# A Perceiver kernel with 64 sequences: context layer norm on VectorE, scores between turned weights and values, first sequences interleaved

## The chip, the cores and the metric

The kernel runs on one core of a Trainium2 chip. The metric is the device time of one execution in microseconds. A core has five engines that run side by side, each through its own queue in order: TensorE (PE, matmuls; PEld are its weight loads), VectorE (DVE), ScalarE (ACT), GpSimd (POOL), and SyncE (SP), which issues most of the DMAs. Matmul results land in PSUM, which the kernel uses as eight banks of 128 x 512 float32.

## What is computed

The reference is two Perceiver layers on `x` (64 sequences of 32 latent tokens, 256 channels) with a context of 257 tokens per sequence. Everything is float32. Cut to what matters here:

```
x += xattn0(layernorm(ctx)*gx+bx, layernorm(layernorm(x))*gl+bl)  # 16 heads of 64; keys and values from
                                                 # context and latents; q and k normed per head
x += attn0(layernorm(x))                         # 16 heads of 16, q and k normed per head
x += moe(layernorm(x))                           # 64 experts, top 8, capacity 128, plus a shared expert
x += xattn1(layernorm(x), ctx)                   # 16 heads of 64
x += attn1(layernorm(x))                         # latent heads of 32, rotary, causal
x += tanh(layernorm(x) @ w @ a1 @ a2 + bias)
```

## The kernel before

Tokens stand in 16 tiles `t` of 128, so a tile holds four sequences (`NB = 4`), and a sequence `s` is number `b = s % 4` of its tile. The program has three parts, called stages here.

**First stage (`before`)**: cross-attention of layer 0 sequence by sequence, and beside it, for tiles that are done, self-attention and routing. For each sequence `CrossFirst` has these steps: `load` (DMA of 256 context rows), `prepare` (layer norm of the context), `turn` (transposition on TensorE, line 1173, and copies to `xT`), `keys` (16 products with `wk`, copies to `kT` by VectorE and ScalarE in turn, and two ScalarE squares `sq` of four head pairs each, line 1206), `norms` (matmuls that sum the squares, line 1218, then a maximum and a logarithm, `nk`), `spread` (matmuls that spread the norms over the rows, line 1239, then four exponentials), `scores` (line 1258, then softmax on VectorE and ScalarE), `weigh` (turns the softmax weights, line 207, copies `at`, line 208), and `values` (line 221, copies `yT`). One pass of the loop works on several sequences: `keys(s+2)`, `weigh(s)`, a slot, `norms(s+2)`, `values(s)`, `spread(s+2)`, a slot, `turn(s+3)`, `scores(s+2)`, `prepare(s+4)`, and, except for a tile's last sequence, a third slot. In a slot every open generator does its next step, up to its next `yield`. A tile's generator `tail` runs `heads_out`, then `self_first` with `attend_self` (line 310 are its values' matmuls, 32 x 32 each), then `route`, which ends in eight indirect DMAs on POOL that scatter the tokens to their experts. The generator `queries` prepares the next tile. The last tile but one is held back by `HOLD` slots.

**Second stage (`experts`)**: 64 experts, with their weights loaded `AHEAD = 12` ahead, and the shared expert between them. In expert 12 the weights of the third stage are loaded and folded (`after_weights`): `latent_weights` and `ffn_weights` each use a temporary pool on the same side of the memory.

**Third stage (`after`)**: layer 1, with `CrossSecond` for the cross-attention and the generator `follow` for output heads, self-attention (`self_second`) and FFN. A pass of the loop is: load, `scores(s+2)`, a slot, `weigh(s)`, a slot, `values(s)`, a slot. The generator `queries(t+2)` joins in the third pass of a tile. `normed`, which both use, makes a layer norm `z` in one step and its transpose `zT` (line 149, copy on line 150) in a later one.

**What sets the order.** The order on TensorE is that of the program (`manual_schedule` for PE). For the other engines and the DMA queues a scheduler picks the order by its own estimate of times; it also chooses between ScalarE and VectorE where the program says `nc.any`, and it may issue a load early once its buffer is free. All PSUM tiles come from one pool of eight banks:

```python
return self.ps.tile([P, 512], F32, name=name, tag="bank")
```

Of the kernel before, what the change touches and what calls it, by code (L numbers as in the profile page):

```python
# [14 lines left out]
ALU = mybir.AluOpType  # L15
AX = mybir.AxisListType

P = 128
D = 256
# [12 lines left out]
AHEAD = 12  # L32
# [54 lines left out]
def done(steps):  # L87
    for _ in steps:
        pass


class Kernel:
# [198 lines left out]
    def attend_self(self, t, e, recip, wo, bias):  # L291

        nc = self.nc
        v = self.vz[t % 2]
        nc.vector.tensor_tensor(e, e, recip.unsqueeze(2).to_broadcast([P, H, S]), ALU.mult)  # L295
        eT = self.wk.tile([P, H, S], F32, name="eT", bufs=self.eb)
        nc.vector.transpose(eT.rearrange("p a b -> p (a b)"), e.rearrange("p a b -> p (a b)"))
        yield
        if self.slack:
            yield  # L300


        ps = [self.bank("psY") for _ in range(NB)]
        for k in range(2):
            for odd in range(2):
                for g in range(4):
                    h = 8 * k + 2 * g + odd
                    for b in range(NB):
                        r = slice(b * S, (b + 1) * S)
                        nc.tensor.matmul(  # L310
                            ps[b][g * 32 : (g + 1) * 32, k * S : (k + 1) * S],
                            lhsT=v[r, h, :, :].rearrange("p a b -> p (a b)"),
                            rhs=eT[r, h, :],
                            start=(odd == 0),
                            stop=(odd == 1),
                        )
        oT = self.wk.tile([P, 2, P], F32, name="oTs", bufs=self.vb)
        for b in range(NB):
            nc.any.tensor_copy(
                oT[:, :, b * S : (b + 1) * S], ps[b][:, : 2 * S].rearrange("p (k i) -> p k i", k=2)  # L320
            )
        yield
        ps = self.bank("psY")
        self.product(ps[:, :D], [oT[:, k, :] for k in range(2)], [wo[:, k, :] for k in range(2)])
        self.add_to_x(t, ps[:, :D], bias)
# [46 lines left out]
    def before(self, ctx):  # L372
# [3 lines left out]
        tc, nc, a = self.tc, self.nc, self.a  # L376
# [3 lines left out]
        w = self.pool(ctx, "w0", 1)  # L380
# [11 lines left out]
        cross = CrossFirst(self, kp)  # L392
# [23 lines left out]
        n = self.nb  # L416
        first = cross.queries(0)
# [2 lines left out]
        next(first)  # L420
        next(first)
        cross.prepare(1)
        for i in range(2):
            cross.load(i + 2)
            cross.turn(i)
            cross.keys(i)
            cross.norms(i)
            done(first)
            cross.spread(i)
            cross.scores(i)  # L430
        cross.load(4)
        cross.prepare(2)
        cross.prepare(3)
        cross.turn(2)

        wv = self.load(w, "wv", [P, 2, HD], a["a_wv"].rearrange("(k p) n -> p k n", p=P))
        wo = self.load(w, "wo", [P, 8, D], a["a_wo"].rearrange("(k p) n -> p k n", p=P))
# [218 lines left out]
    def experts(self, ctx, slot, tails):  # L656
        tc, nc, a = self.tc, self.nc, self.a
        nt = self.nt
        w = self.pool(ctx, "w1", 1)
# [5 lines left out]
        def weigh(e):  # L665
            if e < E:
                t = weights[e] = wk.tile([P, 3 * D], F32, name="we", bufs=AHEAD + 1)
                nc.sync.dma_start(t, a["m_ew"][e])

        def fetch(e):  # L670
            if e < E:
                t = rows[e] = wk.tile([P, D], F32, name="be", bufs=4)
                nc.sync.dma_start(t, self.buf[1 + e * CAP : 1 + (e + 1) * CAP, :])

        def turn(e):
            if e < E:
                t = wk.tile([P, 2, P], F32, name="beT")
                self.transposed(t, rows.pop(e))
                mid[e] = t

        def inner(e):
            if e < E:
                t, we = mid.pop(e), weights[e]
                ps = self.bank("psA")
                for half in range(2):
                    self.product(
                        ps[:, half * P : (half + 1) * P],
                        [we[:, k * D + half * FI : k * D + (half + 1) * FI] for k in range(2)],
                        [t[:, k, :] for k in range(2)],
                    )  # L690
                act = mid[e] = wk.tile([P, P], F32, name="eact")
                nc.scalar.activation(act, ps[:, :P], AF.Silu)
                nc.vector.tensor_tensor(act, act, ps[:, P : 2 * P], ALU.mult)

        def outer(e):
            ps = self.bank("psY")
            self.product(ps[:, :D], [mid.pop(e)], [weights.pop(e)[:, 2 * D :]])
            oe = wk.tile([P, D], F32, name="oe")
            nc.any.tensor_copy(oe, ps[:, :D])
            nc.scalar.dma_start(self.oute[1 + e * CAP : 1 + (e + 1) * CAP, :], oe)  # L700
# [50 lines left out]
        for e in range(E):  # L751
            weigh(e + AHEAD)
            fetch(e + 3)
            turn(e + 2)
            while (at - total + rest) * E < rest * e:
                next(side)
                at += 1
            inner(e + 1)
            outer(e)
            if e == AHEAD:  # L760
                self.after_weights()
        done(side)

        side, sums = shared(nt // GT - 1), self.combine(0)
# [32 lines left out]
    def after_weights(self):  # L797
        a, w = self.a, self.w2
        wq = self.load(w, "wq", [P, 2, HD], a["b_wq"].rearrange("(k p) n -> p k n", p=P))
        wkT = self.load(w, "wkT", [P, 8, D], a["b_wkT"].rearrange("(k p) n -> p k n", p=P))  # L800
        wv = self.load(w, "wv", [P, 2, HD], a["b_wv"].rearrange("(k p) n -> p k n", p=P))
        wo = self.load(w, "wo", [P, 8, D], a["b_wo"].rearrange("(k p) n -> p k n", p=P))
        bo = self.row(w, "bo", a["b_bo"], D)
        self.weights = wq, wkT, wv, wo, bo
        self.lat = self.latent_weights(w)
        self.ffnw = self.ffn_weights(w)

    def after(self, ctx):
        self.eb = self.vb = 1
        self.slack = True  # L810
        nc, n = self.nc, self.nb
        wq, wkT, wv, wo, bo = self.weights
        self.wk = self.wkh = self.pool(ctx, "wk2", 2)
        kp = self.pool(ctx, "kp2", 3)
        cross = CrossSecond(self, kp, wq, wkT, wv, wo, bo)
        for s in range(3):
            cross.load(s)
        second = self.combine(1)
        for _ in range(6):
            next(second)  # L820
        done(cross.queries(0))

        steps = []

        def slot():
            for g in list(steps):
                if next(g, steps) is steps:
                    steps.remove(g)

        cross.scores(0)  # L830
        done(second)
        steps.append(cross.queries(1))
        slot()
        cross.scores(1)
        slot()
        steps.append(self.combine(2, 3))
        for s in range(n):
            t, b = divmod(s, NB)
            if s + 3 < n:
                cross.load(s + 3)  # L840
            if s + 2 < n:
                cross.scores(s + 2)
            if b == NB - 2 and t + 2 < self.nt:
                steps.append(cross.queries(t + 2))
                if t + 3 < self.nt:
                    steps.append(self.combine(t + 3, 3))
            slot()
            cross.weigh(s)
            slot()
            if s < 2:  # L850

                slot()
                slot()
            cross.values(s)
            if b == NB - 1:
                steps.append(self.follow(t, cross.yT, wv, wo, bo))
            slot()
        while steps:
            slot()
# [110 lines left out]
    def self_second(self, t, wl, bl, wvo, bvo, wqk, bqk, wo, bo):  # L970
        nc = self.nc
# [43 lines left out]
        kT = self.wk.tile([P, 4 * P], F32, name="kTl", bufs=1)  # L1015
        nc.any.tensor_copy(kT, ps)
        yield


        ps = [self.bank("psB") for _ in range(4)]  # L1020
# [12 lines left out]
        e = self.wk.tile([P, H, S], F32, name="e", bufs=self.eb)  # L1033
# [45 lines left out]
class CrossFirst:  # L1079
# [76 lines left out]
    def prepare(self, s):  # L1156

        k, nc, cx = self.k, self.k.nc, self.cx[s]
        k.layernorm(cx, cx)
        nc.gpsimd.tensor_tensor(cx, cx, self.gx.unsqueeze(1).to_broadcast([P, 2, D]), ALU.mult)  # L1160
        nc.gpsimd.tensor_tensor(cx, cx, self.bx.unsqueeze(1).to_broadcast([P, 2, D]), ALU.add)

    def turn(self, s):

# [307 lines left out]
```

## Time and profile before

| | |
|---|---|
| median of three runs | 2828.25 us (2827.0 to 2829.42) |
| time of the profiled execution | 2804.67 us |
| its span, first to last instruction | 2802.8 us |
| mean granted TensorE clock | 0.982 |
| PE busy | 2657.6 us (95%) |
| DVE busy | 1694.9 us (60%) |
| ACT busy | 1241.6 us (44%) |
| POOL busy | 684.3 us (24%) |

The first stage lasts until about 1550 us of the span, the second until about 1800, the third to the end. Busy shares are averages over these stages. A row of the timeline has start, duration, engine, line, operation, what it writes and reads, its shape, its count, and in brackets the idle time of the engine before it with what ended it. In a row of the waits stand who waited for whom, the total in us, how often, and the longest. A group of instructions has its busy time in us and the mean in ns of one. The durations come from one profiled execution.

### The profile page before, as it was taken

How to read it: one execution, taken by the hardware profiler on the slowest of the kernel's cores; microseconds unless marked ns; L12 is line 12 of the kernel's file. 1: busy time of each engine (PE TensorE's matmuls, PEld its weight loads, DVE VectorE, ACT ScalarE, POOL GpSimd, SP SyncE). 2: the span in 40 equal slices, each digit the busy share in tenths (PEclk: the TensorE clock that was granted, in tenths of full speed). 3: DMA queues.
4: the chain of work that ended last, by engine and by line, in shares of the span. 5: the costliest groups of instructions: out<-in, count | busy, mean ns of one | idle time of the engine just before them, and what ended most of it. 6: DMA issues, size and time to landing. Idle time of an engine off the chain costs nothing. (4 is left out here: it accounts for less than half of the span.)

```text
span 2802.8 us, 58905 instructions
## 1 busy us (share of the span) xinstructions
PE 2657.6 (95%) x23386; PEld 1824.5 (65%) x23386; DVE 1694.9 (60%) x4427; ACT 1241.6 (44%) x3436; POOL 684.3 (24%) x756
## 2 busy tenths in 40 slices
PE   6999999999999999999999799999999999999996
PEld 3556666666666666666666578667777777777764
DVE  5546666666666666666665433466666666666664
ACT  3455555555555555555554223333333333333331
POOL 5211333133313331243121200321212222121001
PEclk8999999999999999999999899999999999999997
DMA  8000011011000000000001677321211222222110
GB/s 271 16 14 18 31 33 31 18 31 33 29 18 27 26 22 18 20 19 16 18 7 38 233 237 243 91 67 54 58 51 50 59 52 58 56 51 55 33 35 5
DMA packets 136087, 157.03 MB, mean 56 GB/s; under 512 B 24024, under 2 KB 118979, under 8 KB 135812
## 3 DMA queue, kind: packets, MB, share of 16 engines
q1 hardware_dynamic: 114308, 119.65, 13.8%
q0 software_dynamic: 12288, 25.21, 3.4%
q10 hardware_dynamic: 9216, 8.39, 0.9%
q8 instruction: 185, 3.03, 0.4%
q14 instruction: 90, 0.74, 0.1%
HBM read 121.63 MB, written 37.75 MB: 57 GB/s over the span
## 5 line engine op out<-in xcount | busy, mean ns | idle before, releaser
L167 PE MATMUL psA<-xT,wk 128*128 128x289 f32 x2048 | 517.4, 411 | 7.9 <-ACT xT L1176 4.5
L167 PEld LDWEIGHTS psA<-xT,wk 128*128 128x128 f32 x2048 | 388.0, 191 | 134.8 <-issue 21.8
L780 POOL DMA_INDIRECT y<-oute,idx x128 | 131.5, 1028 | 643.4 <-DVE x L791 453.9
L167 PE MATMUL psA<-at,cx 128*128 128x512 f32 x512 | 235.4, 602 | 20.0 <-ACT qTl L1005 18.2
L221 PE MATMUL psY<-at,cx 128*128 128x512 f32 x512 | 239.8, 612 | 0.1
L167 PE MATMUL psY<-xT,qk 128*128 128x257 f32 x1024 | 234.3, 382 | 0.0
L167 PEld LDWEIGHTS psY<-xT,qk 128*128 128x128 f32 x1024 | 190.8, 190 | 35.0 <-issue 10.2
L1357 DVE TENSOR_REDUCE mx<-psY 128x1 f32<-128x257 f32 x256 | 105.7, 423 | 133.6 <-PE psY L167 133.5
L1358 ACT ACTIVATE sim<-psY,mx 128x257 f32<-128x257 f32 x256 | 121.6, 476 | 142.3 <-DVE mx L1357 142.2
L184 ACT ACTIVATE sim<-sim,mx 128x289 f32<-128x289 f32 x256 | 134.1, 526 | 100.0 <-DVE mx L182 100.0
L221 PEld LDWEIGHTS psY<-at,cx 128*128 128x128 f32 x512 | 93.5, 192 | 123.0 <-issue 108.8
L167 PEld LDWEIGHTS psA<-at,cx 128*128 128x128 f32 x512 | 92.9, 190 | 120.8 <-issue 76.7
L233 ACT COPY yT<-psY 128x512 f32<-128x512 f32 x127 | 68.2, 589 | 220.7 <-PE psY L231 220.7
L645 POOL DMA_INDIRECT buf<-z,fi x128 | 126.5, 988 | 148.0 <-DVE fi L642 102.2
L1160 POOL TENSOR_TENSOR cx<-cx,a_gx 128x512 f32<-128x512 f32 x64 | 81.8, 1278 | 292.1 <-DVE cx L140 290.3
L1206 ACT ACTIVATE sq<-kT 128x1156 f32<-128x1156 f32 x128 | 149.4, 1167 | 4.4 <-DVE kT L1203 2.8
L1201 ACT COPY kT<-psA 128x289 f32<-128x289 f32 x256 | 94.8, 389 | 104.2 <-PE psA L167 104.2
L1376 ACT COPY at<-psT 128x512 f32<-128x512 f32 x145 | 78.8, 595 | 123.4 <-PE psT L1375 118.3
L1218 PE MATMUL psB<-sq,c 128*32 128x289 f32 x1024 | 109.4, 419 | 19.7 <-ACT sq L1206 19.5
L1388 DVE SCALAR_TENSOR_TENSOR yT<-at,xT,psA 128x512 f32<-128x512 f32 x128 | 94.0, 735 | 56.1 <-PE psA L167 50.7
L167 PE MATMUL psY<-yT,wv 128*64 128x128 f32 x2048 | 121.6, 275 | 1.6 <-DVE yT L1388 1.4
L1177 POOL COPY xT<-lnT 128x64 f32<-128x64 f32 x64 | 15.3, 240 | 423.0 <-PE psA L167 299.3
(257 smaller groups left out, 5190.5 us busy)
## 6 DMA issues: line engine op xcount, KB each, us to landing
cx<-in_ctx SPq DMA_DIRECT2D x128, 256.0 KB
we<-in_m_ew SPq DMA_DIRECT2D x64, 384.0 KB
xT<-in_ctxT SPq DMA_DIRECT2D x64, 257.0 KB
buf<-zero SPq DMA_DIRECT2D x32, 256.0 KB
be<-buf SPq DMA_DIRECT2D x64, 128.0 KB
oute<-oe ACTq DMA_DIRECT2D x64, 128.0 KB
mu<-in_mask SPq DMA_DIRECT2D x16, 128.5 KB
x<-in_x SPq DMA_DIRECT2D x16, 128.0 KB
```

What stands on the lines that cost most here:

```text
L167: self.nc.tensor.matmul(ps, lhsT=lhs[i], rhs=rhs[i], start=(i == 0), stop=(i == n - 1))
L184: nc.scalar.activation(sim[:, g, :], sim[:, g, :], AF.Exp, bias=mx[:, g : g + 1], accum_out=sm[:, g : g + 1])
L221: nc.tensor.matmul(ps[kc], lhsT=values[i][:, kc * P : (kc + 1) * P], rhs=at[i], start=(i == 0), stop=(i == n - 1 and tail is None),)
L645: d = nc.gpsimd.indirect_dma_start(out=self.buf[:, :], out_offset=bass.IndirectOffsetOnAxis(ap=fi[:, k : k + 1], axis=0), in_=z[:, 0, :], ...
L780: nc.gpsimd.indirect_dma_start(out=y, out_offset=None, in_=self.oute[:, :], in_offset=bass.IndirectOffsetOnAxis(ap=self.idx[:, t, k : k + ...
L1160: nc.gpsimd.tensor_tensor(cx, cx, self.gx.unsqueeze(1).to_broadcast([P, 2, D]), ALU.mult)
L1201: nc.scalar.copy(kT[:, p, :], ps[:, :JK])
L1206: nc.scalar.activation(sq[p // 4], kT[:, p - 3 : p + 1, :], AF.Square)
L1218: nc.tensor.matmul(ps[g * 32 : (g + 1) * 32, :JK], lhsT=k.pair[odd], rhs=sq[p // 4][:, p % 4, :], start=(odd == 0), stop=(odd == 1),)
L1357: nc.vector.tensor_reduce(mx[:, g : g + 1], ps[:, :J], AX.X, ALU.max, negate=True)
L1358: nc.scalar.activation(sim[:, g, :], ps[:, :J], AF.Exp, bias=mx[:, g : g + 1], accum_out=sm[:, g : g + 1])
L1388: nc.vector.scalar_tensor_tensor(self.yT[:, c, :, b * S : (b + 1) * S], self.at[:, 2, :].rearrange("p (h i) -> p h i", h=H), xT[:, c, J - ...
```

## The change

The change has six parts. `prepare` takes mean and scale from `stats` and ends the layer norm with four `scalar_tensor_tensor` of 128 x 256 on VectorE, where two `tensor_scalar` on VectorE and a multiplication and an addition of 128 x 512 on GpSimd stood. `attend_self` gives up its slot once more in the first stage before line 310 (the third stage had that yield already). Before the first stage's loop the first two sequences are interleaved and three contexts are loaded at once. `ffn_weights` moves from expert 12 to expert 24. In the third stage `scores(s+2)` stands behind `weigh(s)` and no longer ahead of the pass's first slot. `self_second` gives up its slot once more before its scores (line 1026).

```diff
--- before.py
+++ after.py
@@ -296,8 +296,7 @@
         eT = self.wk.tile([P, H, S], F32, name="eT", bufs=self.eb)
         nc.vector.transpose(eT.rearrange("p a b -> p (a b)"), e.rearrange("p a b -> p (a b)"))
         yield
-        if self.slack:
-            yield
+        yield
 
 
         ps = [self.bank("psY") for _ in range(NB)]
@@ -420,18 +419,22 @@
         next(first)
         next(first)
         cross.prepare(1)
-        for i in range(2):
-            cross.load(i + 2)
-            cross.turn(i)
-            cross.keys(i)
-            cross.norms(i)
-            done(first)
-            cross.spread(i)
-            cross.scores(i)
-        cross.load(4)
+        for i in range(2, 5):
+            cross.load(i)
+        cross.turn(0)
+        cross.keys(0)
+        done(first)
+        cross.turn(1)
+        cross.norms(0)
         cross.prepare(2)
+        cross.spread(0)
+        cross.scores(0)
+        cross.keys(1)
+        cross.turn(2)
+        cross.norms(1)
         cross.prepare(3)
-        cross.turn(2)
+        cross.spread(1)
+        cross.scores(1)
 
         wv = self.load(w, "wv", [P, 2, HD], a["a_wv"].rearrange("(k p) n -> p k n", p=P))
         wo = self.load(w, "wo", [P, 8, D], a["a_wo"].rearrange("(k p) n -> p k n", p=P))
@@ -759,6 +762,8 @@
             outer(e)
             if e == AHEAD:
                 self.after_weights()
+            if e == 2 * AHEAD:
+                self.ffnw = self.ffn_weights(self.w2)
         done(side)
 
         side, sums = shared(nt // GT - 1), self.combine(0)
@@ -803,7 +808,6 @@
         bo = self.row(w, "bo", a["b_bo"], D)
         self.weights = wq, wkT, wv, wo, bo
         self.lat = self.latent_weights(w)
-        self.ffnw = self.ffn_weights(w)
 
     def after(self, ctx):
         self.eb = self.vb = 1
@@ -838,14 +842,14 @@
             t, b = divmod(s, NB)
             if s + 3 < n:
                 cross.load(s + 3)
-            if s + 2 < n:
-                cross.scores(s + 2)
             if b == NB - 2 and t + 2 < self.nt:
                 steps.append(cross.queries(t + 2))
                 if t + 3 < self.nt:
                     steps.append(self.combine(t + 3, 3))
             slot()
             cross.weigh(s)
+            if s + 2 < n:
+                cross.scores(s + 2)
             slot()
             if s < 2:
 
@@ -1015,6 +1019,7 @@
         kT = self.wk.tile([P, 4 * P], F32, name="kTl", bufs=1)
         nc.any.tensor_copy(kT, ps)
         yield
+        yield
 
 
         ps = [self.bank("psB") for _ in range(4)]
@@ -1156,9 +1161,11 @@
     def prepare(self, s):
 
         k, nc, cx = self.k, self.k.nc, self.cx[s]
-        k.layernorm(cx, cx)
-        nc.gpsimd.tensor_tensor(cx, cx, self.gx.unsqueeze(1).to_broadcast([P, 2, D]), ALU.mult)
-        nc.gpsimd.tensor_tensor(cx, cx, self.bx.unsqueeze(1).to_broadcast([P, 2, D]), ALU.add)
+        mv, rs = k.stats(cx, 2)
+        for j in range(2):
+            x = cx[:, j, :]
+            nc.vector.scalar_tensor_tensor(x, x, mv[:, j, 0:1], self.gx, ALU.subtract, ALU.mult)
+            nc.vector.scalar_tensor_tensor(x, x, rs[:, j : j + 1], self.bx, ALU.mult, ALU.add)
 
     def turn(self, s):
 
```

## The prediction, made before the changed kernel ran

> **What bounds the kernel now.** I read the page first: TensorE is busy nearly throughout, so only its gaps can be won, and whatever is moved out of a gap is lost.
>
> ```profile
> PE 2657.6 (95%) x23386; PEld 1824.5 (65%) x23386; DVE 1694.9 (60%) x4427; ACT 1241.6 (44%) x3436; POOL 684.3 (24%) x756
> ```
>
> Then TensorE's waits in the steady part of the first stage (210 to 1470 us): what waited, for whom, total us, times, longest.
>
> ```profile
> PE psY L310 <- DVE at L208: 14.7, 14, 1.3
> PE psB L1218 <- ACT sq L1206: 9.6, 14, 0.9
> ```
>
> The values' matmuls of self-attention (L310) wait 1.0 us once per tile, for PSUM banks that VectorE still empties. That looks like free time. The timeline of one such iteration (the last sequence of a tile; start, duration, idle before) shows where it sits: turning of weights (L207), L310, key norms (L1218).
>
> ```profile
> 516.41 1.47 PE L207 MATMUL psT<-c,sim 128*128 128x128 f32 x12
> 517.82 0.26 PE L310 MATMUL psY<-eT,vz 32*32 32x32 f32 x6
> 519.10 1.24 PE L310 MATMUL psY<-eT,vz 32*32 32x32 f32 x122 [1.03 <-DVE at L208]
> 520.27 1.86 PE L1218 MATMUL psB<-sq,c 128*32 128x289 f32 x16
> ```
>
> ScalarE in the same iteration, the two squares that the norms read:
>
> ```profile
> 517.13 1.15 ACT L1206 ACTIVATE sq<-kT 128x1156 f32<-128x1156 f32 x1
> ...
> 519.74 1.17 ACT L1206 ACTIVATE sq<-kT 128x1156 f32<-128x1156 f32 x1
> ```
>
> The second ends at 520.91. The norms' first four matmuls (0.44 us) could start at the turns' end (517.88), but the other twelve need that square: they start 0.05 us after it, 3.07 us after the turns' end, and all 14 such iterations show the same to 0.3 us. So the square sets the end here, and L310 with its wait fills the hole before it. What the hole looks like when empty stands in the last sequence of the first tile, which has no self-attention beside it:
>
> ```profile
> 143.42 0.68 PE L1218 MATMUL psB<-sq,c 128*32 128x289 f32 x4
> 146.20 1.26 PE L1218 MATMUL psB<-sq,c 128*32 128x289 f32 x12 [2.10 <-ACT sq L1206]
> ```
>
> and what follows there, cross-attention's values, otherwise 3.70 us for eight:
>
> ```profile
> 147.39 5.26 PE L221 MATMUL psY<-at,cx 128*128 128x512 f32 x8
> ```
>
> In the view by windows the granted clock is 0.5 from 147.14 to 150.56 us: 1.56 us lost after a gap of 2.10 us.
>
> Third stage, one tile: the values wait once per tile for copies on ScalarE (12 tiles, 18.2 us in all); below it a transposed z (L149), today followed by scores.
>
> ```profile
> 2132.73 3.67 PE L167 MATMUL psA<-at,cx 128*128 128x512 f32 x8 [1.50 <-ACT qTl L1005]
> ...
> 2137.53 0.38 PE L149 MATMUL psT<-c,z 128*128 128x128 f32 x2
> ```
>
> Drain and second stage: what a consumer directly behind such a transposition pays, and the wait for the FFN weights.
>
> ```profile
> 1542.53 0.38 PE L149 MATMUL psT<-c,z 128*128 128x128 f32 x2
> 1543.37 0.66 PE L167 MATMUL psA<-gw,zT 128*128 128x65 f32 x4 [0.46 <-ACT zT L150]
> ...
> 1633.27 3.75 PE L167 MATMUL psA<-f_a,f_a1T 128*128 128x256 f32 x8 [4.80 <-DMA f_a<-in_f_a]
> 1636.82 2.86 PE L167 MATMUL psA<-mid,f_wT 128*128 128x256 f32 x8
> ```
>
> Costs of the layer norm's instructions, old and nearest to the new (busy us, mean ns):
>
> ```profile
> L140 DVE TENSOR_SCALAR cx<-cx,mv,rs 128x256 f32<-128x256 f32 x128 | 61.8, 515 | 7.4 <-ACT rs L120 7.4
> ...
> L791 DVE SCALAR_TENSOR_TENSOR x<-y,w,x 128x256 f32<-128x256 f32 x128 | 59.8, 467 | 0.3
> ```
>
> **The change part by part**, against the profiled execution (2804.67 us, span 2802.8; the three runs' median is 2828.25, so I carry the difference over in us).
>
> *One more yield before L310, first stage.* A tile has 11 slots: three per sequence, two for the last. L310 is the tail's tenth step, in the last sequence's slot between turns and norms. It moves one slot on, behind the spread matmuls; later steps move one slot each (product with wo to the next sequence's first slot, then z's turn, gate, count). No DMA moves but zs's store and the scatters on POOL, one slot later; POOL has at most 28 us of work in 70 and TensorE waits for it nowhere here. Now the norms stand directly behind the turns, and their end stays at the square: values still start 4.17 us after the turns. Queued on TensorE behind the waiting norms are values, spread and scores, for which VectorE (nk, then the scores' products) waits in turn, so no other engine uses the hole. L310's 1.42 us (517.82 to 520.27 less 1.03) come out of the hole and are added behind the spread, plus a bank wait like that of L573, which has this place today (2.7 us in 14, 0.19 each), less 0.06 us of wait that the moved count matmuls fill: 1.55 us by 14 tiles = +21.7. Bounds: -12.0, if the square were early and only L310's 14.7 us less 2.7 counted, to +25.
>
> *Clock after the emptied hole.* 0.5 us idle, 0.44 busy, 2.2 idle. [...] of six gaps of 1.98 to 2.39 us outside the end, at full clock (from 53.67, 118.94, 144.10, 1535.06, 1544.03, 1603.30), four were followed by half clock. I take 0.7 by 1.5 us by 14 = +14.7; ends 0 and +21.
>
> *Layer norm on VectorE.* Per sequence two L140 (0.515) and POOL's multiplication and addition (1.28 and 1.27) go; four scalar_tensor_tensor come, by L791 0.467 each: 1.87 - 1.03 = +0.84 us of VectorE, 64 times, 54 us beside an engine 64% busy. POOL's 163 us were off the path, each sequence being prepared an iteration or more ahead. VectorE's queue counts: two of four preparations per tile stand at 569.0 to 571.9, among the copies of turned weights that the values read (last copy 1.60 us after the turns, values at 1.91). Behind them wait these copies and the norms' maximum. [...] POOL keeps one of 3.64 us (mask) and one of 1.92 us (q) per tile. [...] L140 today shows 0.1 us of excess over z's 0.41, so I stay with the rows. On the path I take +3 (0.2 us a tile); ends -1 and +12.
>
> *Start.* keys(1) no longer waits for its turn (0.68 us), but norms(1) still waits for ScalarE's second square at 55.6, behind the softmax of sequence 0. What goes is the turn of sequence 2 and its copy between scores(1) and keys(2) (62.3 to 64.3 us): -2.0, with q's chain freed from POOL -0.8, and spread(0) losing the transposes of q ahead of it +0.5: -2.3. Two cx loads pass four small c3 copies in SP's queue; both landed long before use. Half clock from 54.98 to 68.64 remains, since its waits do; were it gone, -6 more. Ends -8 and +4.
>
> *FFN weights 12 experts later.* Four loads and 16 matmuls move. The loads wait for the memory of the latent weights, free at 1628.1; SP issued later weights up to 36 us ahead of their place, so they pass the queue of expert weights and land long before. The 4.80 us go, and the slow clock behind it (3.75 + 2.86 against twice 1.89): -7.6. Ends: -7.6, and +1 if they keep their place behind expert loads that wait for a slot.
>
> *Third stage.* Scores (16 matmuls, their reduces, exponentials, scaling; no DMA) come between turns and values: the 18.2 us go. But the slots at the end of one iteration and the start of the next now touch. Two consumers stand there directly behind their transposed z: the latent projection (second sequence) and the next queries' projection (last sequence). The drain's row prices it: 0.84 us from start to start where 0.21 suffices, 0.63; at the other, the copy is VectorE's from 2137.96 to 2138.38, behind another: 0.71. 14 tiles by 1.34 = 18.8. The yield added before L1026 keeps that one from joining them. Net +0.6; ends -18 and +10.
>
> *Last tiles:* one empty step more, 0 (-3 to +3). Sum: 21.7 + 14.7 + 3 - 2.3 - 7.6 + 0.6 = +30.1, or 2858.
>
> **Rivals.** (a) The clock holds[...]: +15, 2844. For it: 18 us of 1.5 us gaps never slowed it. (b) Faster: without L310's banks in between, the second square lands early. It decides at 1.5 us after the turns, against 3.02 today: then L310's wait is won, and the sum is -12.0 - 2.3 - 7.6 + 0.6 = -21, 2807. Against it: nothing of L310 stands ahead of that square on ScalarE, which runs without pause from 515.04 to 520.91. (c) VectorE becomes the bound: 0.84 us late in most norms or values, some 20 us more, 2877. Against it: it idles 6 us in each iteration. (d) The gains of start and third stage are at their better ends and cancel the rest: within 6 us. (e) "Ended on VectorE" moves nothing, because the instructions find idle time: inside the main case.
>
> **How the numbers follow.** Main case 0.42, (a) 0.22, (c) 0.10, (d) 0.10, (b) 0.16. A measurement here tells about 0.2% (5.7 us) from no change. Slower: 0.42 + 0.22 + 0.10 = 0.74; same 0.10; faster 0.16. Range 2814 to 2878: it leaves out most of (b) and the upper end of (c).
>
> **What would show it.** L1218 waiting some 2.2 us for the square in each tile's last sequence, L310 behind L1239 with at most 0.2 us of wait, half-clock stretches once per tile; in the third stage no wait of values, but 0.5 us waits for zT (L150) twice per tile; no wait for f_a. The forecast is wrong if the second square ends within 1.5 us of the turns, or if the first stage's period falls below today's 93.6 us a tile.

## The result and the profile after

The kernel after takes 2928.06 us (median of four runs, 2923.61 to 2929.26), beside 2827.62 us of the kernel before on the same chip: a ratio of 1.0353, 95% interval 1.0341 to 1.0365. That is 100 us slower. The forecast was 30 us slower, 2858, and its range ended at 2878.

The page's line of the engines. TensorE's busy time grew by 46.5 us and its share fell from 95% to 92%; POOL lost 157 us and VectorE took 48.

```profile
PE 2704.1 (92%) x23386; PEld 1837.7 (63%) x23386; DVE 1742.7 (60%) x4544; ACT 1241.6 (42%) x3447; POOL 527.7 (18%) x628
```

TensorE's waits in the steady part of the first stage, 210 to 1540 us (who waited for whom, total us, times, longest). Before, the squares cost 9.6 us here in 14 waits. L1140 are the transpositions of q; "issue" means that the trace shows nothing that they waited for.

```profile
PE psB L1225 <- ACT sq L1213: 52.2, 51, 2.0
PE psT L1140 <- issue: 25.7, 38, 1.2
PE psA L167 <- issue: 5.8, 16, 0.9
```

The timeline of a tile's last sequence on TensorE, and the second square on ScalarE (start, duration, idle before), the place of the forecast's first two steps:

```profile
636.31 1.47 PE L207 MATMUL psT<-c,sim 128*128 128x128 f32 x12
638.23 0.68 PE L1225 MATMUL psB<-sq,c 128*32 128x289 f32 x4 [0.45 <-ACT sq L1213]
640.86 1.48 PE L1225 MATMUL psB<-sq,c 128*32 128x289 f32 x12 [1.95 <-ACT sq L1213]
642.26 5.04 PE L221 MATMUL psY<-at,cx 128*128 128x512 f32 x8
...
648.30 0.77 PE L1246 MATMUL psR<-nk,c 32*128 32x289 f32 x8
649.00 0.28 PE L309 MATMUL psY<-eT,vz 32*32 32x32 f32 x6
649.53 1.42 PE L309 MATMUL psY<-eT,vz 32*32 32x32 f32 x122 [0.24 <-ACT yT L233]
```

```profile
639.64 1.17 ACT L1213 ACTIVATE sq<-kT 128x1156 f32<-128x1156 f32 x1
```

The square ends at 640.81 and the norms go on 0.05 us later, 3.08 us after the turned weights: the hole is as forecast. Self-attention's values stand behind the spread norms with 0.24 us of wait, and the values of cross-attention take 5.04 us instead of 3.70: the granted clock is 0.50 from 641.59 to 645.00. That part happened as written.

What was not forecast stands two iterations earlier, in the tile's second sequence. TensorE, and then POOL in the same microseconds (the eight scatters, L648):

```profile
601.02 1.20 PE L1265 MATMUL psB<-kT,qTf 64*32 64x289 f32 x32
602.16 0.33 PE L1140 MATMUL psT<-c,q 128*128 128x128 f32 x1
603.20 0.27 PE L1140 MATMUL psT<-c,q 128*128 128x128 f32 x1 [0.72 <-issue]
603.93 0.27 PE L1140 MATMUL psT<-c,q 128*128 128x128 f32 x1 [0.46 <-issue]
604.65 0.31 PE L1140 MATMUL psT<-c,q 128*128 128x128 f32 x1 [0.45 <-issue]
606.08 0.49 PE L1140 MATMUL psT<-c,q 128*128 128x128 f32 x3 [1.11 <-issue]
606.83 0.27 PE L1140 MATMUL psT<-c,q 128*128 128x128 f32 x1 [0.27 <-issue]
607.55 1.80 PE L167 MATMUL psA<-xT,wk 128*128 128x289 f32 x3 [0.45 <-issue]
```

```profile
596.03 1.08 POOL L648 DMA_INDIRECT buf<-z,fi  x1 [5.45 <-DVE junk L637]
...
605.09 0.97 POOL L648 DMA_INDIRECT buf<-z,fi  x1 [0.30 <-issue]
```

Eight transpositions that take 1.1 us elsewhere take 4.9 here, and keys then run at a mean granted clock of 0.69: the view by windows (columns: busy us of PE, PEld, DVE, ACT and POOL, then the granted clock) shows the stalled stretch and the one behind it.

```profile
602.16:607.55 5.39, 1.94 (x17) 0.98 (x9) 1.64 (x4) 1.14 (x4) 4.03 (x7) 0.99 0.27 97
607.55:612.99 5.44, 5.44 (x16) 4.08 (x17) 5.01 (x8) 2.25 (x6) 2.31 (x2) 0.69 0.00 0
```

In before the scatters of such a tile ran from 564.62 to 574.65, over keys, turned weights, norms and values, and were done five microseconds before the burst of scores:

```profile
564.62 1.08 POOL L645 DMA_INDIRECT buf<-z,fi  x1 [7.86 <-DVE fi L642]
...
573.68 0.97 POOL L645 DMA_INDIRECT buf<-z,fi  x1 [0.30 <-issue]
```

```profile
579.48 1.20 PE L1258 MATMUL psB<-kT,qTf 64*32 64x289 f32 x32
```

One slot later they lie over that burst and the transpositions of q.

The other steps. Third stage: the values wait for nothing, and transposed z and the product with wv do:

```profile
2253.26 0.38 PE L149 MATMUL psT<-c,z 128*128 128x128 f32 x2
2254.38 3.84 PE L167 MATMUL psA<-zT,wq 128*128 128x128 f32 x32 [0.73 <-ACT zT L150]
...
2270.86 3.71 PE L167 MATMUL psY<-yT,wv 128*64 128x128 f32 x62 [0.46 <-DVE yT L1395]
```

The FFN weights' matmuls wait no more (before: 4.80 us, and durations of 3.75 and 2.86 us, now 1.89 and 2.19):

```profile
1779.98 1.89 PE L167 MATMUL psA<-f_a,f_a1T 128*128 128x256 f32 x8
```

The layer norm's four new instructions (busy us, mean ns) take 0.99 us for each half of a context, where the forecast had 0.93:

```profile
L1168 DVE SCALAR_TENSOR_TENSOR cx<-cx,rs,a_bx 128x256 f32<-128x256 f32 x128 | 62.1, 508 | 3.9 <-issue 1.1 <-ACT rs L120 1.1 <-DVE cx L1167 0.4
L1167 DVE SCALAR_TENSOR_TENSOR cx<-cx,mv,a_gx 128x256 f32<-128x256 f32 x128 | 60.4, 484 | 0.0
```

### The profile page after: what moved, and what is told of

Same layout as the page of the kernel before. It is cut to its first block, busy times and chain, and to the rows that moved or that the text cites. A ratio compares the mean times of both kernels' runs of the same rounds, so it can differ in the third digit from the quotient of the medians.

```text
span 2926.4 us, 59052 instructions
## 1 busy us (share of the span) xinstructions
PE 2704.1 (92%) x23386; PEld 1837.7 (63%) x23386; DVE 1742.7 (60%) x4544; ACT 1241.6 (42%) x3447; POOL 527.7 (18%) x628
## 4 chain that ended last, share of the span: by engine, by line
PE 69%; DVE 16%; ACT 9%; issue 4%; DMA 1%; POOL 0%; another core or an unknown queue 0%; SPq 0%; DVEq 0%; POOLq 0%; ACTq 0%
PE psA L167 23%; PE psY L167 17%; PE psY L221 9%; PE psB L1225 3%; PE psT L1382 3%; ACT sq L1213 2%; PE psY L231 2%; PE psB L1265 2%; DVE sim L1274 2%; ACT sim L184 2%; DVE sim L1275 2%; PE psY L309 1%; PE psA L1325 1%; PE psB L167 1%; DVE mx L182 1%
## 5 line engine op out<-in xcount | busy, mean ns | idle before, releaser
L167 PE MATMUL psA<-xT,wk 128*128 128x289 f32 x2048 | 530.8, 416 | 9.8 <-issue 6.5
L221 PE MATMUL psY<-at,cx 128*128 128x512 f32 x512 | 256.1, 646 | 3.4 <-ACT at L208 3.4
L221 PEld LDWEIGHTS psY<-at,cx 128*128 128x128 f32 x512 | 100.1, 207 | 142.6 <-issue 115.8
L1225 PE MATMUL psB<-sq,c 128*32 128x289 f32 x1024 | 115.6, 449 | 64.9 <-ACT sq L1213 64.9
L1213 ACT ACTIVATE sq<-kT 128x1156 f32<-128x1156 f32 x128 | 149.0, 1164 | 12.1 <-DVE kT L1210 10.5
L1274 DVE TENSOR_TENSOR sim<-psB,sim 128x289 f32<-128x289 f32 x256 | 102.6, 448 | 79.0 <-PE psB L1265 26.8
L648 POOL DMA_INDIRECT buf<-z,fi x128 | 128.1, 1001 | 115.6 <-DVE junk L637 75.6
L1383 ACT COPY at<-psT 128x512 f32<-128x512 f32 x130 | 71.1, 586 | 133.1 <-PE psT L1382 76.9
L167 PEld LDWEIGHTS psY<-yT,wv 128*64 128x64 f32 x2048 | 115.0, 137 | 19.1 <-DVE yT L1395 11.2
L1210 DVE COPY kT<-psA 128x289 f32<-128x289 f32 x256 | 109.9, 449 | 25.6 <-PE psA L167 25.5
```

The costliest lines, as they stand in the source:

```text
L167: self.nc.tensor.matmul(ps, lhsT=lhs[i], rhs=rhs[i], start=(i == 0), stop=(i == n - 1))
L221: nc.tensor.matmul(ps[kc], lhsT=values[i][:, kc * P : (kc + 1) * P], rhs=at[i], start=(i == 0), stop=(i == n - 1 and tail is None),)
L648: d = nc.gpsimd.indirect_dma_start(out=self.buf[:, :], out_offset=bass.IndirectOffsetOnAxis(ap=fi[:, k : k + 1], axis=0), in_=z[:, 0, :], ...
L1210: nc.vector.tensor_copy(kT[:, p, :], ps[:, :JK])
L1213: nc.scalar.activation(sq[p // 4], kT[:, p - 3 : p + 1, :], AF.Square)
L1225: nc.tensor.matmul(ps[g * 32 : (g + 1) * 32, :JK], lhsT=k.pair[odd], rhs=sq[p // 4][:, p % 4, :], start=(odd == 0), stop=(odd == 1),)
```

## The experiments

Six comparisons were run, each on one chip with the kernel before beside it. They fall into two kinds, and without this no number below can be read. In three, the median of the kernel before is 2822 to 2829 us; I call these crowded. In the other three it is 2801 to 2804 us; I call these quiet. The names are labels and say nothing of a cause: no run tells what differs, or whether the chip or the moment decides. The kernel after's times above are crowded; the profile of before that the forecast rests on (2804.67 us) is a quiet one. Ratios are to before in the same comparison.

**The yield undone.** In the kernel after:

```diff
-        yield
+        if self.slack:
+            yield
         ps = [self.bank("psY") for _ in range(NB)]
```

> The kernel after with one edit undone: the conditional yield before attend_self's values, as before. Theory S (the yield costs it all: it empties the hole behind the turns, about 2.6 us per tile, and it moves the scatters under the burst of scores and the transposes of q, about 5.6 us per tile): 2928 - 14 x 8.2 = 2813 us, 2805 to 2825, and no stretch in which the transposes of q (L1140) wait. Theory V (the layer norm on VectorE causes the waits of L1140): the 5.6 us stay, 2928 - 14 x 2.6 = 2892 us.

Quiet: 0.9968, interval 0.9956 to 0.9981. Within theory S (2805 to 2825 us are 0.992 to 0.999), and the yield is what makes the change a loss. The waits of L1140 are gone, but since this comparison was quiet that alone tells nothing (see the unchanged kernel below).

**Two more yields ahead of the scatters.** In the kernel after:

```diff
+        yield
+        yield
         for k in range(TOPK):
             d = nc.gpsimd.indirect_dma_start(
```

> The kernel after with two more yields, placed directly before the loop of eight scatters, so that they are issued at the end of an iteration, beside keys and turned weights, and not between spread and scores. Theory S: the waits of L1140 and the half clock behind them go, the hole behind the turns stays: 2928 - 14 x 5.6 = 2850 us, 2840 to 2862. Theory V: no change, 2928 us within 6.

Quiet: 1.0212 (1.0190 to 1.0233), 60 us. The edit did not do what it was for: the scatters start 5.00 us ahead of the scores' burst, as in after. Only TensorE's order is the program's; POOL's is picked by the scheduler. Yet L1140 waited nowhere, with the same order around it. So the conditions have to be compared with the kernel unchanged, which is done below.

**The yield alone**, in the kernel before, and **the layer norm on POOL again**, in the kernel after. The first was run three times, the second twice.

```diff
-        if self.slack:
-            yield
+        yield
         ps = [self.bank("psY") for _ in range(NB)]
```

```diff
-        mv, rs = k.stats(cx, 2)
-        for j in range(2):
-            ...
+        k.layernorm(cx, cx)
+        nc.gpsimd.tensor_tensor(cx, cx, self.gx.unsqueeze(1).to_broadcast([P, 2, D]), ALU.mult)
+        nc.gpsimd.tensor_tensor(cx, cx, self.bx.unsqueeze(1).to_broadcast([P, 2, D]), ALU.add)
```

> The kernel before with one edit only: the unconditional second yield before attend_self's values. Theory S: 2828 + 14 x 8.2 = 2943 us, 2930 to 2955, with L1140's counterpart waiting beside the scatters. Theory V: only the hole and its clock, 2828 + 14 x 2.6 = 2864 us.

> The kernel after with one edit undone: the contexts' layer norm ends on POOL again (two tensor_scalar on VectorE, a multiplication and an addition on POOL). Theory S: the waits of L1140 stay, 2928 us within 12. Theory V: they go, 2928 - 14 x 5.6 = 2850 us. POOL's 2.55 us per sequence come back into its queue; if the scatters are pushed later by them, the waits can move too.

> The kernel before with the unconditional yield alone, again, now to be read against after on the same chip. Theory Y (the yield alone places the scatters under the burst, the layer norm has no part): waits of q's transposes as in after, 1.035 + 0.004 to 0.008 where before takes 2822 us or more (the gains of start and FFN weights are missing). Theory B (both edits are needed: POOL's layer norm operations of 1.28 us ahead of the scatters keep them off): 1.019 as before, no such waits.

> The kernel after with the layer norm's end on POOL, again, beside after. Theory Y: 1.035 within 0.004. Theory B: 1.018.

> The kernel before with the unconditional yield alone, a third time. Where before takes 2822 us or more: theory Y (the yield alone puts the scatters where they disturb) 1.035 to 1.045 with waits of q's transposes; theory B (only with the layer norm on VectorE) 1.016 to 1.020 and no such waits. Where before takes 2800 to 2804 us: 1.0185 again.

All five quiet. Yield alone: 1.0190, 1.0184 and 1.0199, 51 to 56 us. Layer norm on POOL: 1.0184 and 1.0206. No waits of L1140 in any. The numbers I expected of either theory missed: 1.019 lies between "only the hole" (1.013) and "hole and scatters" (1.041). Whether the yield alone, without VectorE's layer norm, also brings the waits of L1140 in a crowded comparison stays open, as all three runs of it were in quiet ones.

**The kernels unchanged.** After three more times, before once for its profile.

> The kernel after, unchanged, once more beside the kernel before. The kernel with two more yields ahead of the scatters (e2_scat2) left the order beside the scatters as in after, and its transposes of q (L1140) waited nowhere. Theory A (the waits belong to the arrangement, and e2 broke them by chance): ratio 1.035 again, period 102 us per tile. Theory R (the waits come and go between runs on different chips for one and the same program): ratio 1.02, 1.017 to 1.024, the period 98 us, and no waits of L1140.

> The kernel after, unchanged. Theory A (the waits of L1140 belong to the arrangement): 1.035 of before wherever it runs. Theory R (they depend on the chip): 1.035 where before takes 2828 us, 1.02 where it takes 2804 us.

> The kernel after, unchanged, to read the three others against on the same chip. Theory R: 1.035 of before where before takes 2822 to 2829 us, 1.02 where it takes 2804 us.

> The kernel before, unchanged, for its profile beside the others of this call. Where the runs of before take 2828 us, theory R expects a period of 95 us per tile here, the added time in the second sequence's iteration, beside the scatters; where they take 2804 us, 93.6.

After: 1.0350 (crowded), 1.0348 (crowded), 1.0210 (quiet, 2862.16 us, interval 1.0193 to 1.0227). So one and the same program is 3.5% slower on the one kind and 2.1% on the other, and in the quiet profile the waits without a cause are nearly gone:

```profile
PE psB L1225 <- ACT sq L1213: 59.8, 55, 1.9
...
PE psB L1265 <- issue: 2.2, 3, 1.1
```

The kernel before in a crowded profile (span 2822.7, quiet 2802.8) shows a wait just behind the scatters that its quiet profile lacks, in nine tiles, in eight of them 12.4 us after the first scatter:

```profile
PE psR L1239 <- ACT nk L1227: 11.6, 9, 1.4
```

The four iterations of a tile, from one start of turned weights to the next, mean of tiles 2 to 13, in us (b0 is the tile's first sequence):

| kernel | kind | b0 | b1 | b2 | b3 | tile |
|---|---|---|---|---|---|---|
| before | quiet | 29.50 | 21.87 | 20.62 | 21.60 | 93.6 |
| before | crowded | 29.50 | 22.77 | 20.52 | 21.60 | 94.4 |
| yield alone (second run) | quiet | 29.87 | 22.97 | 20.98 | 23.29 | 97.1 |
| after | quiet | 29.87 | 22.90 | 21.55 | 24.12 | 98.4 |
| after (first profile) | crowded | 29.87 | 27.26 | 20.76 | 24.52 | 102.4 |
| after without scatters | crowded | 29.87 | 22.73 | 21.23 | 23.98 | 97.8 |

What crowding adds to after is 4.0 us a tile: 4.4 in b1, beside the scatters, of which b2 gains some back. The other two crowded profiles of after have 101.8 and 102.1 us a tile.

**The scatters left out.** In the kernel after the loop of eight scatters is dropped, so that the experts compute on zeros.

```diff
-        for k in range(TOPK):
-            d = nc.gpsimd.indirect_dma_start(
-            ...
```

> The kernel after with the eight scatters of each tile left out (the rows of the experts stay zero, so the experts compute on zeros; all other instructions stay). If the scatters cause the waits of L1140 and what follows them: no such waits, the period near 97.3 us as with the layer norm on POOL, so 14 x (102.3 - 97.3) = 70 us less than after where after shows the waits, and within 10 us of it where it does not. If the burst of scores alone causes them: no change.

Crowded: 1.0109 (1.0092 to 1.0126), against 1.0348 of after in the same comparison: 67 us less, 70 expected. Waits in the same window as above (L1213 are the norms here, L1253 the scores):

```profile
PE psB L1213 <- ACT sq L1201: 57.7, 55, 1.9
...
PE psB L1253 <- issue: 2.1, 3, 0.9
```

The span, 2852.1, is that of a quiet run (2863.7) and a little less. So the waits of L1140 are caused by the scatters, and the burst of scores alone does not cause them.

**The hole filled.** In the kernel after, two matmuls whose result nobody reads:

```diff
             slot()
+            if b == NB - 1 and s + 2 < n:
+                ps = self.bank("psF")
+                for _ in range(2):
+                    nc.tensor.matmul(ps, lhsT=self.ident, rhs=wq[:, 0, :512], start=True, stop=True)
             if s + 2 < n:
                 cross.norms(s + 2)
```

> The kernel after with two matmuls (128x512, result unused) put into each tile's last sequence between the turned weights and the key norms, where the yield left a hole. They take 1.85 us by the row of the values, in a hole of 2.2 to 2.6 us. If the half clock behind the hole is the hole's doing, the work is free and gives back the clock: 14 x 1.4 = 20 us less than after. If the clock falls for another reason: no change, or up to 14 x 0.3 = 4 us more.

Crowded: 1.0287 (1.0265 to 1.0308) against 1.0348: 17 us faster by the ratios, 14 by the medians, with 28 us of work added (15 times 1.88; the trace has two records for each of the two matmuls). TensorE in the last sequence:

```profile
628.99 1.47 PE L207 MATMUL psT<-c,sim 128*128 128x128 f32 x12
630.30 1.88 PE L501 MATMUL psF<-wq,c 128*128 128x512 f32 x4
632.11 0.68 PE L1229 MATMUL psB<-sq,c 128*32 128x289 f32 x4
633.54 1.17 PE L1229 MATMUL psB<-sq,c 128*32 128x289 f32 x12 [0.74 <-ACT sq L1217]
634.64 3.70 PE L221 MATMUL psY<-at,cx 128*128 128x512 f32 x8
```

The values take 3.70 us again, and b3 loses no clock in any of 14 tiles. In the three crowded profiles of after it loses 1.71 us in 10 to 13 of 14 tiles, in the quiet one in 10, and with the yield alone in 6 or 7.

**The third stage alone**, in the kernel before:

```diff
-            if s + 2 < n:
-                cross.scores(s + 2)
             ...
             cross.weigh(s)
+            if s + 2 < n:
+                cross.scores(s + 2)
             slot()
@@ self_second
         nc.any.tensor_copy(kT, ps)
         yield
+        yield
```

> The kernel before with the third stage's edits alone: scores between turned weights and values, and the yield ahead of self-attention's scores. The prediction's sum: +0.6 us, from -18.2 of waits that go and +18.8 of new waits for zT; the milestones of the two traces say +8.8. Theory Z (the waits for zT are all that comes): ratio 1.000, within 0.0015. Theory M (the milestones): 1.003.

Crowded: 1.0039 (1.0025 to 1.0053), 11 us slower: theory M. TensorE's waits in the third stage up to its last tiles (1803 to 2790 us):

```profile
PE psA L167 <- ACT zT L150: 15.7, 27, 0.7
PE psT L149 <- DVE z L140: 8.1, 2, 6.4
PE psY L167 <- DVE yT L1389: 7.3, 15, 0.9
PE psA L167 <- DVE zT L150: 1.7, 1, 1.7
```

In before's profile the same part (1786 to 2760 us) had 18.2 us of waits for qTl, 5.3 for z and 1.4 for yT, and 0.5 for zT.

**The layer norm on VectorE alone**, in the kernel before (the diff of `prepare` as in the change):

> The kernel before with the layer norm's end on VectorE alone. The prediction: +3 us, between -1 and +12. From e1 (period 93.20 us per tile against 93.58): 14 x -0.38 = -5 us, ratio 0.998.

Crowded: 0.9954 (0.9937 to 0.9971), 13 us faster. The first turned weights come at 68.4 us instead of 74.0, and from there to the last tile's first turned weights it is 8.4 us shorter. Not all of this is the layer norm: 5.1 of the first 5.5 us and 3.4 of the 8.4 are half clock that this profile does not have.

**The scatters later.** In the kernel after, POOL work in the chain of the scatters' indices:

```diff
-        nc.vector.tensor_copy(fi, far)
+        late = self.wk.tile([P, 1024], F32, name="late", bufs=1)
+        nc.gpsimd.memset(late, 1.0)
+        nc.gpsimd.tensor_copy(late[:, :TOPK], far)
+        for _ in range(3):
+            nc.gpsimd.tensor_scalar(late, late, 1.0, None, ALU.mult)
+        nc.gpsimd.tensor_copy(fi, late[:, :TOPK])
```

> The kernel after with some 4 to 12 us of POOL work (a memset, two copies and three tensor_scalar on a 128x1024 tile) in the chain that makes the scatters' indices, so that the eight scatters start that much later, under the keys and no longer under the burst of scores and the transposes of q. Nothing else moves. Theory P (place): the waits of L1140 go, 1.012 to 1.016 of before where after is 1.035. Theory E (eight scatters cost TensorE the same wherever they stand): 1.035.

Quiet: 1.0530. It does not tell P from E, since after is 1.021 there. It shows another price instead. The multiplication of self-attention's q and k (L543) is queued on POOL behind the scatters, and TensorE waits for it:

```profile
PE psT L555 <- POOL qk L543: 48.3, 12, 4.9
```

```profile
619.88 0.97 POOL L653 DMA_INDIRECT buf<-z,fi  x1 [0.31 <-issue]
620.84 0.98 POOL L646 MEMSET late<- 128x1024 f32 x1
...
622.06 0.72 POOL L543 TENSOR_TENSOR qk<-qk,sg 128x256 f32<-128x256 f32 x1
```

**A version that beats both.** The kernel after without the first stage's yield and without the third stage's edits; layer norm on VectorE, interleaved start and later FFN weights stay. Run twice:

> The kernel after without the yield in the first stage and without the third stage's edits: layer norm on VectorE, interleaved start and later FFN weights stay. If the third stage costs 8.8 us in after: 0.9968 - 0.0031 = 0.9937 of before. If it costs nothing: 0.997.

> The kernel after without the yield in the first stage and without the third stage's edits, again. 0.9918 where before took 2828.86 us; where before takes 2800 to 2804 us, from e1 (0.9968 with the third stage's edits, which cost 0.0031 to 0.0039): 0.993.

Crowded 0.9918 (0.9900 to 0.9936), quiet 0.9931 (0.9914 to 0.9949): 23 and 19 us faster than before. Against the version with the third stage's edits (0.9968, quiet) it is 10 us better. It is also the one changed kernel besides after that ran in both kinds, and it keeps after's layer norm and start: crowding costs its span 22.5 us (2807.1 against 2784.6) and its tile 1.0 us (94.25 against 93.21), without a wait of q's transpositions.

## Why the prediction was wrong

It missed by 70 us. Stages by the profiles, in us (starts of the first turned weights, of the first expert's transposition, of the first scores of layer 1, end of the last matmul; the span ends 8.7 us later):

| | before, quiet | after, quiet | before, crowded | after, crowded |
|---|---|---|---|---|
| start | 74.3 | 66.8 | 74.0 | 68.0 |
| rest of the first stage | 1514.1 | 1579.1 | 1532.3 | 1640.3 |
| second | 197.3 | 192.2 | 199.5 | 192.1 |
| third | 1008.4 | 1016.8 | 1008.1 | 1017.3 |
| span | 2802.8 | 2863.7 | 2822.7 | 2926.4 |

Like with like, the change costs 60.9 us quiet and 103.7 crowded. The first is 30.8 over the sum of +30.1. The rest of the miss is that the forecast carried the difference between profile and median (23.6 us) over unchanged. It is what crowding costs: 19.9 us in before's spans, 62.7 in after's. So of the 70 us some 40 are crowding that the change made worse, and 30 are terms that were mis-sized.

**The step that failed most**: "No DMA moves but zs's store and the scatters on POOL, one slot later; POOL has at most 28 us of work in 70 and TensorE waits for it nowhere here". The step costed a moved transfer by POOL's idle time, and so at nothing. In crowded runs the scatters stall TensorE where they meet the transpositions of q behind the burst of scores: leaving them out saves 67 us of 2822. It is the yield that makes crowding so dear: the version without the yield and the third stage's edits, with the scatters in their old place, pays 22.5 us of crowding where after pays 62.7 (1.0 us a tile where after pays 3.4 to 4.0). Quiet, TensorE's waits in after show no cost of the scatters: none of L1140, where the crowded profile has 25.7 us.

That the place makes the difference is in part argued, as no crowded run moved the scatters alone. What speaks for it is before's crowded profile. There VectorE too stands still beside the scatters, in 14 tiles and for 2.7 to 4.8 us, before an operation whose norms TensorE had ended at 665.4 (in the quiet profile once):

```profile
670.49 0.46 DVE L1226 TENSOR_SCALAR nk<-psB 128x289 f32<-128x289 f32 x1 [4.77 <-PE psY L231]
```

TensorE is meanwhile in the values, 3.70 and 1.13 us of long matmuls, and of such a stall at most 1.4 us comes through to it. Behind the burst of scores it has only the short transpositions, 0.27 to 0.33 us each where they stand alone in the stall above, and these come late one by one, with 0.27 to 1.11 us of idle time before them.

**The yield, mis-sized.** The forecast had 1.55 us per tile without the clock. The yield alone, quiet, is 97.11 - 93.58 = 3.53 us per tile, of which 0.57 is clock: 2.96, or 41 us for 14 tiles instead of 21.7 (the other two profiles of it give 2.8). The 1.42 us of L310 were counted rightly. The forecast let each later step find a place of the same worth ("less 0.06 us"). In b0 this holds: its 0.37 us are matmuls that moved there, with no wait. In b1 the values start 1.05 us later, 0.80 of it because the second square ends 1.57 us after the turned weights instead of 0.77; in b2 the square is 0.36 us later. With b3's hole the waits for the square are 55 in place of 14, in three of four sequences.

In b1 VectorE's last copy of keys, which the square needs, runs behind statistics of the next context. The first of these, an instruction of 128 x 2 that takes 0.15 us in before, takes 1.88, from the moment that POOL multiplies q (yield alone, second run):

```profile
578.66 1.88 DVE L118 TENSOR_SCALAR rs<-mv 128x2 f32<-128x2 f32 x1
```

```profile
578.58 1.92 POOL L1123 TENSOR_TENSOR q<-q,ss 128x1024 f32<-128x1024 f32 x1 [10.85 <-ACT ss L1122]
```

The pair meets in 14 or 15 of 16 tiles of every profile with this yield, and in one tile of before's. In two crowded profiles without the yield, those of the layer norm alone and of the version that beats both, it meets in 9 or 10 tiles, but 9 us later, well behind the last copy of keys, and the square is not late. The forecast had named POOL's q of 1.92 us under the layer norm and had added nothing for it; the overlap came by the yield instead. That POOL holds VectorE up here is read from the overlap, as no run took q's multiplication away; what delays b2's square stays open.

**The clock, right.** 14.7 us forecast, as 0.7 of 14 gaps. In after's quiet profile the last sequence loses clock in 10 of 14 tiles, 17 us; with the yield alone in 6 or 7, 10 to 12 us. Filling the hole gave back 14 to 17. The longest gap of the hole is 1.95 us, with 0.45 idle and 0.68 busy ahead of it, and the clock halved in 6 to 13 of 14 tiles, so rival (a) falls. Rival (b) falls with the square at 3.02 to 3.05 us after the turned weights in every profile.

**The layer norm, wrong in sign where it stands alone.** Forecast +3 within -1 and +12; alone it is 13 us faster (crowded, interval 8 to 18). Part of that is clock: its four runs were granted 0.984 to 0.987, those of before beside it 0.981 to 0.985. In the steady tiles, where neither profile loses clock, it gains 0.27 us a tile crowded (94.13 against 94.40), and 0.38 quiet in the kernel with the yield undone (93.20 against 93.58): 4 to 5 us, where the forecast had lost 0.2 a tile. Quiet, this is b2's wait for the square, 9.6 us before and half of that now:

```profile
PE psB L1226 <- ACT sq L1214: 4.8, 14, 0.4
```

So VectorE's added work found idle time; why the square comes earlier is not shown. Beside the yield the gain is used up: 2862.16 against 2859.07 us with POOL's version. VectorE's price was near (0.99 against 0.93 per half). Rival (c) did not come: VectorE is no busier than 62% in any profile.

**The start** came 7.5 us earlier, 2.3 forecast, and the difference is the clock. The forecast let the half clock stand ("Half clock from 54.98 to 68.64 remains"); before has half clock for 17.1 us of its start, after's quiet profile for 6.8, which is 5.1 us of lost time less. The other 2.4 are the forecast's. How much half clock a start meets varies where no edit touches the start: in those profiles the first turned weights come at 70.2 to 74.3 us.

**FFN weights**: the wait is gone, the second stage is 5.1 us shorter quiet and 7.4 crowded, 7.6 forecast.

**Third stage**: +0.6 forecast, +8.4 measured, 11 alone. The 18.2 us went, and zT's waits came to 17.4 where 18.8 was expected. Two things were missing. One is the product with wv directly behind the values, 15 waits of some 0.5 us where 1.4 us stood, and the longest wait for z, 6.4 us instead of 4.1. The other is the end of the stage, which the forecast put at 0 ("one empty step more"): there self-attention's values wait longer for eT. The rows to the end of the last matmul, before and after (quiet):

```profile
PE psY L310 <- DVE eT L297: 8.7, 2, 7.5
```

```profile
PE psY L309 <- DVE eT L297: 14.2, 2, 7.4
```

All rows of waits to that end sum to 43.4 us before and to 53.2 after, while half clock takes 2.8 us less.

**Last tiles** of the first stage: 0 forecast; the drain behind the last full tile is 2.0 us longer.

## What to carry to other kernels

A step that gives up its slot moves every later step of its chain, and each of them has to be looked up where it lands: on TensorE, whether it now fails to cover a wait; on the other queues, what its transfers lie over. The time in which TensorE waits for a fixed event is worth filling: here two matmuls of 1.88 us together fitted into the wait for the square, and the kernel became 14 us faster than after; left empty, the hole was followed by 1.71 us of lost clock in 10 to 13 of 14 tiles. Before an effect is added to a median, look whether profile and median come from the same conditions: here 24 us of difference was itself an effect that the change tripled.

## What the runs showed of the hardware

One program has two levels of time: the kernel before took 2798 to 2807 us in all runs of the quiet comparisons and 2821 to 2832 us in all runs of the crowded ones. The level can be read from a profile. The records of the scatters' completions have gaps in crowded profiles: of 128 per tile, 19 to 51 are left in the first 14 tiles of every crowded profile that has scatters, and 111 to 128 in every quiet one.

In the stall TensorE's starts come in steps of about 0.72 or 1.43 us (603.20, 603.93, 604.65, 606.08, 606.83, 607.55), and for none of them does the profile name anything that they wait for. VectorE's products of the scores wait as well although the scores were done at 602.2: they start at 607.60, after 3.21 us that the profile puts down to L1140, and in tile 4 (counted from 0), where L1140 does not stall, there is a hole of 2.45 us in them. No run shows what holds these starts up, so the cause below the scatters stays open.
